# The sort of the edges moved into the first convolution of a graph network, with other changes to scatters and small products

## The chip, the cores and the metric

One core of one Trainium2 chip runs the kernel. The metric is device time in microseconds, the median of several executions. A core has five engines that run their own instruction streams in order: TensorE (PE: matrix products into PSUM), VectorE (DVE), ScalarE (ACT), GpSimd (POOL) and SyncE (SP, which here only issues transfers). They meet through semaphores. Transfers are issued from the queues of SP, ACT and POOL and are carried out by 16 DMA engines.

## The reference

There are 12500 nodes with 64 features and 200000 edges, sorted by `dst`. Two GraphSAGE convolutions are followed by one edge network with a mean over the edges of each source node:

```python
h = relu(layernorm(x))
# twice, a relu between the two:
#   mean of h[src] over the edges of each dst, then  mean @ Wl.T + b + h @ Wr.T
x = x + conv2(relu(conv1(h)))
h = relu(layernorm(x))
# edge network
inp = concatenate([h[src], h[dst], edge_attr], axis=-1)
msg = relu(inp @ W1 + b1) @ W2 + b2
x = x + segment_mean(msg, src)
```

The kernel splits the first product of the edge network: `h[src] @ W1[0:64]` and `h[dst] @ W1[64:128]` are formed per node, and `edge_attr @ W1[128:192]`, the *edge terms*, per edge.

## The kernel before

**Blocks and cells.** The nodes are cut into NB = 49 blocks of 256. A *cell* is a pair (block of dst, block of src); there are 49 x 49 = 2401 cells, and a cell has room for S = 128 edges. For each cell the kernel holds the source's and the target's number inside its block. Gathering rows of a block is then a product with a one-hot matrix (`turned`, lines 640 to 650, made by VectorE from rows of numbers that are broadcast to all partitions), and summing over targets is another such product (`hot`, lines 652 to 661, made from columns of numbers).

**Start.** `find_blocks` finds for each block the window of the sorted edges that holds its own, `begin_i`. `features` (433) makes the layer norm of all nodes and splits it into three bf16 parts, the table `ta`. Meanwhile SP's queue gets transfers that write zeros into four tables `terms[0..3]` in DRAM (`zeros`, 250), 832 KB each.

**The sort** (`cells`, 464, in a pool scope of its own). `edges_in` (501) loads source and target numbers for seven blocks of dst at a time (14 transfers on SP's queue). `sort(B)` (536) does one block in five stages: one-hot of the source block for the window's 128 x 34 places (540), counts per column by 34 products (546), a running sum (550), the rank of each edge inside its cell by products with a triangular matrix (558, 559) and a minimum over PSUM (563), a compare of ranks with 0..127 (569), 34 products that put the numbers in place (579), three transfers of the result to DRAM (584 to 586), and a transpose for the column form (589 to 591). It also writes `pos`, the place in `terms` for each edge's term. Blocks are staggered: the loop at 599 runs the stages of several blocks in each turn. After 18 blocks it has issued all zeros and begins to run the edge terms beside the sort.

**The edge terms** (`edge_terms`, 321) come in *units* of up to four items, an item being 128 x 2 edges of one block: transposes (368), a copy by ACT (373), products with the weights (380), a copy by ACT into one of four buffers `terms_o` (388), and then one indirect scatter per item and half, on POOL's queue (345), into table `B % 4`. Blocks are taken four at a time, one for each table, and block 48 alone. In all there are 49 x 34 = 1666 scatters. A unit is emitted in six steps; `Beside` (394) holds a pace, and whoever calls `passed(us)` advances the steps that have come due. So the order of work is that of the program, written out by hand: each engine's queue gets instructions in the order in which the Python code emits them.

**The convolutions** (loop at 846). For `layer` 0 and 1, cells in order, 16 to a part, four to a turn. A turn calls `some_cells` (792): it emits the gather products of four cells (801), their copies into a ring of seven row buffers (805; `RB`, 269) and the one-hot of the targets (806); three turns later the sums' products (681) into the block's PSUM bank `acc`. After the last cell of a block `conv` (718) goes on: it copies the sums (722), forms the mean (726 to 734), transposes it and multiplies it by the weights in the bank `pX` (738, 744), and `after_conv1` or `after_conv2` finishes. Every turn also advances the edge terms: `beside.passed((z - a) * 0.37)` in layer 0, 0.375 in layer 1, against a pace of 10.4/6 for a step. `wait_rows` (634) loads the rows of a part, two parts ahead, through SP.

**The last stage** (loop at 972) gathers from both tables, adds the edge terms that come back from `terms`, applies relu, sums and finishes each node.

Of the kernel before, what the change touches and what calls it, by code (L numbers as in the profile page):

```python
# [9 lines left out]
FT = mybir.dt.float32  # L10
BF = mybir.dt.bfloat16
# [103 lines left out]
def fast_path(  # L115
# [39 lines left out]
    BIG = 1024.0  # L155
# [35 lines left out]

    per = EROWS * D // P
    ZW = per // NB
    zero = consts.tile([P, ZW], FT, name="zero")
    nc.gpsimd.memset(zero, 0.0)
# [54 lines left out]
    def zeros():  # L250

        n = 2
        for k in range(0, NB, n):
            m = min(n, NB - k)
            for j in range(J):
                nc.sync.dma_start(terms[j].rearrange("(p n r) d -> p n (r d)", p=P, n=NB)[:, k:k + m],
                                  zero.unsqueeze(1).to_broadcast([P, m, ZW]))
                yield

    clearing = zeros()  # L260
# [8 lines left out]
    RB = 7  # L269
# [51 lines left out]
    def edge_terms(work, psum):  # L321

        loads = []
        for q in (*range(BJ - 3), BJ - 1, BJ - 3, BJ - 2):
            blocks = range(q * J, min(q * J + J, NB))
            step = 3 if len(blocks) == J else 4
            loads += [(blocks, t0, min(step, TG - t0)) for t0 in range(0, TG, step)]

        def load(blocks, t0, m):
            n = len(blocks)  # L330
            e = work.tile([P, J, 3, 2 * D], FT, name="edges")
            ev = e.rearrange("p j c d -> p (j c) d").rearrange("p (a c) d -> p a c d", a=n if n == J else 1)
            for i, B in enumerate(blocks):
                s = nc.sync.value_load(begin_i[0:1, B:B + 1], min_val=0, max_val=E - WIN)
                a = edge[bass.ds(s, WIN)].rearrange("(p t) d -> p t d", t=T)
                nc.sync.dma_start(ev[:, i, 0:m].rearrange("p c d -> p (c d)"),
                                  a[:, 2 * t0:2 * (t0 + m)].rearrange("p t d -> p (t d)"))
            return ev

        def scatter(o, blocks, unit):  # L340
            for h in range(2):
                for c, (i, tg, _) in enumerate(unit):
                    B = blocks[i]
# [12 lines left out]
        for at, (blocks, t0, m) in enumerate(loads):  # L356
            n = len(blocks)
            ev = ahead

            if n == J:  # L360
                units = [[(i, t0 + c, ev[:, i, c]) for i in range(n)] for c in range(m)]
            else:
                units = [[(0, t0 + c, ev[:, 0, c]) for c in range(m)]]
            for u, unit in enumerate(units):
# [22 lines left out]
                o = work.tile([P, 4, 2, D], FT, name="terms_o", bufs=4)  # L387
                nc.scalar.copy(o[:, :k], pm[:, :k])
                before = scatter(o, blocks, unit)
# [43 lines left out]
    def features():  # L433
# [6 lines left out]
        with tc.tile_pool(name="in", bufs=3) as work:  # L440
            line = Line()
            for s in range(NB // CH):
                line.tick(some(work, s))
                next(finding, None)
                next(clearing, None)
                line.tick()
                next(finding, None)
                next(clearing, None)
            while line.all:
                line.tick()  # L450
                next(finding, None)
                next(clearing, None)
            for _ in finding:
                pass

    features()
    first.close()
    psum_x = ctx.enter_context(tc.tile_pool(name="psum_x", bufs=1, space=bass.MemoryType.PSUM))
# [3 lines left out]
    beside = Beside(edge_terms(terms_work, psum_x), 10.4 / 6)  # L462

    def cells():
        work = stage.enter_context(tc.tile_pool(name="cells", bufs=2))
# [780 lines left out]
```

## Time and profile before

| | us |
|---|---|
| median of 3 runs (4303.64 to 4310.11) | 4305.94 |
| the profiled execution | 4318.44 |
| its span, first to last instruction | 4316.5 |

A page of the profile begins with busy time per engine:

```
PE 3760.4 (87%) x50387; PEld 3550.8 (82%) x50387; DVE 3400.7 (79%) x6079; ACT 2487.0 (58%) x5687; POOL 2704.7 (63%) x2300
```

PEld is the loading of weights, which overlaps the products. The first gather product of the first convolution starts at 806.8 us of the span, that of the second at 1765.4, the last stage's first product at 2848.9. A group line of the profile reads: line, engine, operation, out<-in, shapes, count | busy us, mean ns of one | idle us ahead of them, and what ended that idle time. Rows of the sort's operations, from the stretch 0 to 830 us:

```
L579 PE MATMUL pC<-hot_r,hot 128*98 128x128 bf16 x1666 | 162.0, 282 | 16.9 <-ACT dcol L591 16.8
L569 DVE TENSOR_TENSOR hot_r<-rank_b,rexp 128x4352 bf16<-128x4352 bf16 x49 | 118.8, 2425 | 1.7
L563 DVE TENSOR_REDUCE rank<-pR 128x10 f32<-128x490 f32 x147 | 93.1, 663 | 87.4 <-PE pR L559 87.1
L558 PE MATMUL pR<-hot,lead 128*128 128x490 bf16 x147 | 75.4, 513 | 0.0
L559 PE MATMUL pR<-wide,ones 49*128 49x490 bf16 x147 | 74.8, 509 | 0.0
L546 PE MATMUL pH<-ones,hot 128*49 128x1 bf16 x1666 | 62.1, 172 | 83.1 <-DVE before L550 47.0 <-issue 36.0
L540 DVE TENSOR_TENSOR hot<-kv,kexp 128x1666 bf16<-128x1666 bf16 x49 | 50.0, 1020 | 52.7 <-PE pC L579 52.7
L558 PE MATMUL pR<-hot,lead 128*128 128x196 bf16 x49 | 15.5, 316 | 0.0
L559 PE MATMUL pR<-wide,ones 49*128 49x196 bf16 x49 | 15.4, 315 | 0.0
L589 PE MATMUL pC<-ident_b,rows_o 98*128 98x98 bf16 x49 | 12.6, 258 | 0.0
```

and of the edge terms, from 810 to 1760 us:

```
L380 PE MATMUL pE<-we,edges_t 128*128 128x128 f32 x675 | 91.9, 279 | 0.0
L368 PE MATMUL pE<-ident,edges 128*128 128x128 f32 x340 | 52.6, 277 | 4.0 <-ACT terms_o L388 4.0
L388 ACT COPY terms_o<-pE 128x512 f32<-128x512 f32 x85 | 51.0, 600 | 6.8 <-DMA terms<-terms_o,pos 6.4
```

### The profile page before, as it was taken

To read this page: it belongs to the slowest core of one execution; us is meant where nothing else is said; L and a number is where in the kernel's file an instruction comes from. 1 tells how busy PE (TensorE), PEld (TensorE's weight loads), DVE (VectorE), ACT (ScalarE), POOL (GpSimd) and SP (SyncE) were. 2 spreads that over 40 slices of the span, in tenths; PEclk is the share of its full clock that TensorE was granted. 3 is DMA by queue.
4 is the path that set the end of the run, shared out by engine and by line. 5 is a ranking of instruction groups with operands and counts; after the bars stand their busy time and mean duration, and the time that the engine had idled before them with its cause. 6 is when DMAs were issued, how large, how long until landed. Compare 5 with 4: busy or idle time off the path is not lost.

```text
span 4316.5 us, 124949 instructions
## 1 busy us (share of the span) xinstructions
PE 3760.4 (87%) x50387; PEld 3550.8 (82%) x50387; DVE 3400.7 (79%) x6079; ACT 2487.0 (58%) x5687; POOL 2704.7 (63%) x2300
## 2 busy tenths in 40 slices
PE   0767767699999999999998899979999989999997
PEld 0445545699999999999998799978898989888987
DVE  6878666477777777777776677879999999999997
ACT  2001111366666666667665566656676767776775
POOL 3008888777777777777775677725555555554554
PEclk9957666799999999999999899989999999999999
DMA  5971111343444344444443344355554545454552
GB/s 208 358 280 46 45 47 43 104 133 122 135 130 132 127 132 130 125 141 132 133 125 111 107 131 130 121 185 163 168 178 160 179 168 178 164 173 160 176 177 98
DMA packets 309532, 620.93 MB, mean 144 GB/s; under 512 B 74402, under 2 KB 158630, under 8 KB 308864
## 3 DMA queue, kind: packets, MB, share of 16 engines
q1 hardware_dynamic: 247572, 557.98, 39.3%
q0 software_dynamic: 53312, 51.36, 4.1%
q8 instruction: 396, 6.49, 0.6%
q10 hardware_dynamic: 8060, 3.53, 0.3%
q14 instruction: 192, 1.57, 0.1%
HBM read 465.04 MB, written 150.96 MB: 143 GB/s over the span
## 4 chain that ended last, share of the span: by engine, by line
PE 54%; issue 12%; DVE 11%; POOL 10%; DMA 4%; ACT 2%; SPq 1%; POOLq 0%; ACTq 0%; DVEq 0%
PE acc L681 20%; PE got L801 13%; POOL terms L345 10%; PE got L919 10%; PE got L920 5%; DMA terms<-terms_o,pos 3%; PE pE L380 3%; DVE turned_d L647 3%; DVE turned L647 2%; DVE hot L656 1%; PE pE L368 1%; DVE y L925 1%; DVE mean L880 1%; PE pX L744 1%; ACT rows L805 1%
## 5 line engine op out<-in xcount | busy, mean ns | idle before, releaser
L345 POOL DMA_INDIRECT terms<-terms_o,pos x1666 | 1898.3, 1139 | 803.0 <-issue 462.9
L805 ACT CAST rows<-got 128x384 bf16<-128x384 f32 x2402 | 1035.5, 484 | 578.8 <-PE got L801 568.4
L932 POOL TENSOR_TENSOR hidden<-hidden 128x512 f32<-128x512 f32 (+1 forms) x602 | 771.5, 1281 | 723.6 <-ACT hidden L929 700.0
L681 PEld LDWEIGHTS <-hot 128*128 128x128 bf16 x12006 | 1045.9, 99 | 46.3 <-issue 30.5
L681 PE MATMUL acc<-rows,hot 128*128 128x193 bf16 x9604 | 1008.8, 247 | 2.2 <-DVE hot L656 2.2
L647 DVE TENSOR_SCALAR turned<-srow,nid 128x2048 bf16<-128x2048 bf16 (+1 forms) x906 | 756.7, 849 | 124.7 <-PE got L801 116.7
L919 PE MATMUL got<-tb,turned_d 128*128 128x128 bf16 x4802 | 755.1, 223 | 85.6 <-DVE turned_d L647 85.6
L801 PEld LDWEIGHTS <-turned 128*128 128x128 bf16 x9604 | 813.2, 98 | 7.5 <-issue 6.3
L656 DVE TENSOR_TENSOR hot<-dcol,local 128x1024 bf16<-128x1024 bf16 x1202 | 798.1, 684 | 22.7 <-PE acc L681 22.1
L919 PE MATMUL got<-ta,turned 128*128 128x128 bf16 x4802 | 744.9, 223 | 23.2 <-DVE y L926 16.1
L920 PE MATMUL got<-tb,turned_d 128*128 128x64 bf16 x4802 | 686.2, 195 | 0.0
L920 PE MATMUL got<-ta,turned 128*128 128x64 bf16 x4802 | 678.8, 195 | 0.0
L919 PEld LDWEIGHTS <-turned_d 128*128 128x128 bf16 x4802 | 449.5, 100 | 101.3 <-DVE turned_d L647 97.5
L940 ACT ACTIVATE hot_a<-every,less 128x256 bf16<-128x256 bf16 x1200 | 507.7, 495 | 0.0
L801 PE MATMUL got<-ta,turned 128*128 128x192 bf16 x4802 | 495.4, 246 | 6.1 <-issue 5.8
L801 PE MATMUL got<-tb,turned 128*128 128x192 bf16 x4802 | 496.8, 247 | 0.0
L919 PEld LDWEIGHTS <-turned 128*128 128x128 bf16 x4802 | 450.6, 99 | 35.3 <-DVE y L926 27.3
L920 PEld LDWEIGHTS <-turned_d 128*128 128x128 bf16 x4802 | 447.1, 99 | 0.0
L920 PEld LDWEIGHTS <-turned 128*128 128x128 bf16 x4802 | 445.7, 99 | 0.0
L941 ACT ACTIVATE hot_a<-hot_a 128x1024 bf16<-128x1024 bf16 x300 | 317.5, 1058 | 9.5
L647 DVE TENSOR_SCALAR turned_d<-drow,nid 128x2048 bf16<-128x2048 bf16 (+1 forms) x302 | 309.7, 1068 | 1.9 <-DMA drow<-drow_k 1.9
L929 ACT ACTIVATE hidden<-y 128x512 f32<-128x512 f32 (+1 forms) x301 | 190.0, 631 | 206.2 <-DVE y L926 190.8
(206 smaller groups left out, 4912.8 us busy)
## 6 DMA issues: line engine op xcount, KB each, us to landing
srow<-srow_b SPq DMA_DIRECT2D x300, 512.0 KB
terms<-zero SPq DMA_DIRECT2D x96, 832.0 KB
srow<-srow_k SPq DMA_DIRECT2D x150, 512.0 KB
drow<-drow_k SPq DMA_DIRECT2D x150, 512.0 KB
terms_in<-terms SPq DMA_DIRECT2D x147, 384.0 KB
edges<-in_edge_attr_dram SPq DMA_DIRECT2D x240, 192.0 KB
terms<-terms_o,pos POOLq DMA_INDIRECT x1666
terms_in<-terms SPq DMA_DIRECT2D x49, 416.0 KB
```

Source lines behind the costliest of these rows:

```text
L345: nc.gpsimd.indirect_dma_start(out=terms[B % J][:], out_offset=bass.IndirectOffsetOnAxis(ap=pos[:, B, t:t + 1], axis=0), in_=o[:, c, h], i ...
L647: nc.vector.tensor_scalar(o[:, h, :n * S], r[:, :n * S], nid[:, h:h + 1], None, op0=OP.is_equal)
L656: nc.vector.tensor_tensor(o[:, :n], cols.rearrange("p (g c) -> p g c", c=2).unsqueeze(2).to_broadcast([P, n, 2 * P, 2]), local.rearrange(" ...
L681: nc.tensor.matmul(self.acc[B][:, h, :W3], lt, r[:, c, 0:W3], start=k + h == 0, stop=k == NB - 1 and h == 1, skip_group_check=True)
L801: nc.tensor.matmul(p[:, (i - c) * D3:(i - c + 1) * D3], t[:, h, (a - c0 + i) * S:(a - c0 + i + 1) * S], table[:, (a + i) % NB, h], start=h ...
L805: nc.scalar.copy(g[:, c:c + m, :D3], p[:, :m * D3].rearrange("p (c d) -> p c d", c=m))
L919: nc.tensor.matmul(p[:, c], lt, rt[:, 0:2 * D], start=i == 0, stop=False, skip_group_check=True)
L920: nc.tensor.matmul(p[:, c, 0:D], lt, rt[:, 2 * D:], start=False, stop=i == 3, skip_group_check=True)
L929: nc.scalar.activation(w[:, :n, 0:D], y[:, :n], AF.Relu)
L932: nc.gpsimd.tensor_sub(w[:, :n, (i + 1) * D:(i + 2) * D], w[:, :n, j], upper(w)[:, :n, j])
L940: nc.scalar.activation(q[:, c - k], every, AF.Abs, bias=less[(a + c) // NB][:, (a + c) % NB:(a + c) % NB + 1])
L941: nc.scalar.activation(q[:, :n - k], q[:, :n - k], AF.Relu, bias=1.0, scale=-2.0)
```

## The change

The sort has no stage of its own any more. `made_cells` is a generator of 12 steps a block; block 0 is sorted ahead of the first convolution, and the other 48 in its turns, by `sort_to(z)`, about one block per row of 49 cells and one to two blocks ahead. Its tiles have one buffer each, its PSUM is the one bank `pX`. The minimum over PSUM becomes four copies by ACT, two halving minima and one reduction by VectorE; the compare of ranks is done in two halves. The overflow check uses the counts.

Zeros: two tables are cleared at the start, all 50 transfers ahead of `features` in SP's queue; the other two are cleared in the first convolution, one transfer every eight cells. The zeros are now read from the end of `tb`, the table of the second convolution, which has moved to the constants.

Edge terms: none beside the sort. Blocks 0 to 11 are taken in pairs of two tables (0 and 1 first, then 2 and 3), the rest in fours, the last five together. The buffers `terms_o` go from four to three, `RB` from seven to five. A turn passes 1.1 per cell in layer 0 and 0.9 in layer 1 against a pace of 3.64 for a step.

The small products of `conv` go into its own bank `acc`, behind the sums that have been copied out, and no longer into `pX`. Layer 1's temporary tiles come from a pool that is opened when the sort's is closed. Block 0's edge numbers are loaded through ACT's queue.

```diff
+    tb = consts.tile([P, NB, 2, D3], BF, name="tb")
-    zero = consts.tile([P, ZW], FT, name="zero")
-    nc.gpsimd.memset(zero, 0.0)
+    ZB = -(-ZW // D3)
+    nc.vector.memset(tb[:, NB - ZB:], 0.0)
+    zero = tb[:, NB - ZB:].rearrange("p b h d -> p (b h d)").bitcast(FT)[:, :ZW]
...
-    def zeros():
+    def zeros(tables):
...
-            for j in range(J):
+            for j in tables:
...
-    clearing = zeros()
+    EARLY = 2
+    clearing = zeros(range(EARLY))
...
-    RB = 7
+    RB = 5
...
     def edge_terms(work, psum):
+        groups = [[q, q + 1] for q in range(0, 3 * J, J)] + [[q + 2, q + 3] for q in range(0, 3 * J, J)]
+        groups += [[*range(q, q + J)] for q in range(3 * J, NB - 1 - J, J)]
+        q = NB - 1 - J
+        groups.append([q, q + 1, q + 4, q + 2, q + 3])
+        ITEMS = 12
         loads = []
-        for q in (*range(BJ - 3), BJ - 1, BJ - 3, BJ - 2):
-            blocks = range(q * J, min(q * J + J, NB))
-            step = 3 if len(blocks) == J else 4
+        for blocks in groups:
+            step = ITEMS // len(blocks)
             loads += [(blocks, t0, min(step, TG - t0)) for t0 in range(0, TG, step)]
...
+            items = [(B, t0 + c, e[:, i * m + c]) for c in range(m) for i, B in enumerate(blocks)]
+            units = [items[u:u + 4] for u in range(0, len(items), 4)]
...
-                o = work.tile([P, 4, 2, D], FT, name="terms_o", bufs=4)
+                o = work.tile([P, 4, 2, D], FT, name="terms_o", bufs=3)
...
+    for _ in clearing:
+        pass
     features()
     first.close()
+    clearing = zeros(range(EARLY, J))
...
         def sort(B):
...
+            nc.vector.tensor_tensor(v[:, :, 0], mid(pairs(kv), NB), lead_(kexp, TG), op=OP.is_equal)
+            yield
+            many = psum.tile([P, 512], FT, name="pX")
             for g in range(TG):
                 for c in range(2):
-                    nc.tensor.matmul(many[:, 2 * g + c:2 * g + c + 1], v[:, g, 0, :, c], ones[:, 0:1],
+                    nc.tensor.matmul(many[:NB, 2 * g + c:2 * g + c + 1], v[:, g, 0, :, c], ones[:, 0:1],
                                      start=True, stop=True)
+            nc.vector.tensor_tensor_scan(b[:, 1:T + 1], flat_ones, many[:NB, :T], 0.0, op0=OP.mult, op1=OP.add)
             yield
...
+            for n, g0 in enumerate(range(0, TG, 5)):
+                yield
...
+                nc.tensor.matmul(q, lead, flat(v[:, g0:g1, 0]), start=True, stop=False)
+                nc.tensor.matmul(q, ones[:NB], flat(w[:, g0:g1]), start=False, stop=True)
+                nc.scalar.copy(flat(r[:, g0:g1]), q)
+                if n < 2:
+                    nc.vector.tensor_mul(v[:, :, n + 1], v[:, :, 0], mid(pairs((slo, dlo)[n]), NB))
             yield
+            k = NB
+            for _ in range(2):
+                h = k - k // 2
+                nc.vector.tensor_tensor(r[:, :, 0:k - h], r[:, :, 0:k - h], r[:, :, h:k], op=OP.min)
+                k = h
+            nc.vector.tensor_reduce(pairs(rank), r[:, :, 0:k].rearrange("p g k c -> p g c k"), AX.X, OP.min)
...
+            for n, (g0, g1) in enumerate(((0, (TG + 1) // 2), ((TG + 1) // 2, TG))):
+                hot = work.tile([P, (TG + 1) // 2, S, 2], BF, name="hot_r", bufs=1)
+                nc.vector.tensor_tensor(hot[:, :g1 - g0], mid(pairs(rb)[:, g0:g1], S), lead_(rexp, g1 - g0),
+                                        op=OP.is_equal)
+                yield
...
+    STEPS = 12
+    sorted_to = [0]
...
+    sorter = made_cells(sorting.enter_context(tc.tile_pool(name="cells", bufs=2, side="right")), psum_x)
+    while sorted_blocks() < 1:
+        next(sorter)
+
+    def sort_to(a):
+        while sorter is not None and sorted_to[0] < STEPS * (1 + min((a + 4) / 14, 1 + (a + 12) / NB)):
+            if next(sorter, sorter) is sorter:
+                break
+
+    beside = Beside(edge_terms(terms_work, psum_x), 3.64)
...
     def conv(layer, table, w, b, finish, B, acc):
...
-        pt = psum_x.tile([P, 4, P], FT, name="pX")
         for h in range(2):
-            nc.tensor.transpose(pt[:, h], m[:, h].rearrange("p a d -> p (a d)"), ident)
+            nc.tensor.transpose(acc[:, h, :P], m[:, h].rearrange("p a d -> p (a d)"), ident)
...
-        po = psum_x.tile([P, 8, D], FT, name="pX")
         for h in range(2):
-            nc.tensor.matmul(po[:, h], ct[:, h], w, start=True, stop=True)
+            nc.tensor.matmul(acc[:, h, P:P + D], ct[:, h], w, start=True, stop=True)
...
+    sort_to(0)
+    filled = 0
...
             line.tick(some_cells(layer, t, c0, a, z))
+            if layer == 0:
+                sort_to(z)
+                while filled < z:
+                    filled += 8
+                    next(clearing, None)
             next(coming, None)
-            beside.passed((z - a) * (0.37, 0.375)[layer])
+            beside.passed((z - a) * (1.1, 0.9)[layer])
...
+        if layer == 0 and c1 == CELLS:
+            for _ in chain(sorter, clearing):
+                pass
+            sorting.close()
+            second[0] = layers.enter_context(tc.tile_pool(name="second", bufs=2))
```

## The prediction

> **What bounds the kernel now.** I began with the busy rows of the page, then the table of busy time by stretch, then the scatters (line 345) by stretch, then the waits, then the timeline. The busy rows, in 40 slices of 108 us:
>
> ```profile
> PE   0767767699999999999998899979999989999997
> POOL 3008888777777777777775677725555555554554
> GB/s 208 358 280 46 45 47 43 104 133 122 135 130 132 127 132 130 125 141 132 133 125 111 107 131 130 121 185 163 168 178 160 179 168 178 164 173 160 176 177 98
> ```
>
> There are three regimes: zeroing and sorting (to 324 us), sorting with scatters (to 807), the rest. The table by stretch (us; PE, PEld, DVE, ACT, POOL busy; clock; DMA share; GB/s):
>
> ```profile
> 324.00:807.00 483.00, 332.65 (x2916) 244.18 (x2915) 299.32 (x444) 68.12 (x182) 390.66 (x303) 0.67 0.19 48
> 807.00:1765.00 958.00, 953.38 (x10906) 945.22 (x10906) 700.73 (x1384) 658.78 (x1611) 742.15 (x684) 1.00 0.42 129
> 2306.00:2414.00 108.00, 72.96 (x717) 69.73 (x715) 51.08 (x118) 46.91 (x127) 37.36 (x35) 0.81 0.29 88
> 2849.00:4316.00 1467.00, 1324.82 (x24157) 1289.05 (x24155) 1366.05 (x2038) 1008.52 (x1899) 771.45 (x602) 0.97 0.50 167
> ```
>
> The stretch from 807 to 1765 is the first convolution; PE is full there. POOL looks 77% busy, but its group lines for 430 to 800, 807 to 1765 and 2306 to 2414 say otherwise:
>
> ```profile
> L345 POOL DMA_INDIRECT terms<-terms_o,pos x238 | 298.9, 1256 | 72.6 <-issue 70.4 <-DMA terms<-terms_o,pos 1.2 <-ACT rows_o L582 0.9
> L345 POOL DMA_INDIRECT terms<-terms_o,pos x684 | 742.8, 1086 | 216.0 <-issue 191.9 <-DMA terms<-terms_o,pos 10.4 <-ACT rows L805 8.2
> L345 POOL DMA_INDIRECT terms<-terms_o,pos x35 | 37.5, 1072 | 70.9 <-DMA terms<-terms_o,pos 58.1 <-ACT terms_o L388 5.8 <-issue 3.2
> ```
>
> In the second line 742.8 + 216.0 = 958.8 us: POOL has no free time, its idle time is 0.3 us of issue ahead of each scatter. In the first, 298.9 + 72.6 = 371 of 370. So from 324.1 us, where the first scatter starts, to about 2802, where the last ends, POOL runs one scatter after another: 1666 in 2478 us, 1.49 each (1.56 beside the sort, 958/684 = 1.40 in the first convolution, 541/375 = 1.44 in the second up to 2306). Whatever is done to the sort, the last stage (from 2849) can't begin before this queue is done. **So I count scatters, and check the other engines against that count.**
>
> Two things lengthen a scatter. Here one meets a long VectorE compare:
>
> ```profile
> 712.21 2.43 DVE L569 TENSOR_TENSOR hot_r<-rank_b,rexp 128x4352 bf16<-128x4352 bf16 x1
> 712.96 2.52 POOL L345 DMA_INDIRECT terms<-terms_o,pos  x1 [0.30 <-issue]
> 715.78 1.20 POOL L345 DMA_INDIRECT terms<-terms_o,pos  x1 [0.30 <-issue]
> ```
>
> The scatter, 0.97 us when free, ends 0.84 after the compare does (714.64): it stood still while the compare ran. The other is its table. From 2306 to 2414 block 48 is scattered alone, all into one table:
>
> ```profile
> 2311.69 0.97 POOL L345 DMA_INDIRECT terms<-terms_o,pos  x1 [1.46 <-DMA terms<-terms_o,pos]
> 2314.96 0.97 POOL L345 DMA_INDIRECT terms<-terms_o,pos  x1 [2.30 <-DMA terms<-terms_o,pos]
> 2319.54 1.09 POOL L345 DMA_INDIRECT terms<-terms_o,pos  x1 [3.61 <-DMA terms<-terms_o,pos]
> 2323.73 1.30 POOL L345 DMA_INDIRECT terms<-terms_o,pos  x1 [3.10 <-DMA terms<-terms_o,pos]
> ```
>
> Each waits until the one before it has landed. Start to start is 2.40 to 5.25 us, 3.16 on average over the 33 steps there. With four tables in turn this wait is 10.4 us in 684 scatters.
>
> **Head.** The 483 us with scatters and most of the 324 ahead go. Kept: features, zeros for two tables, block 0. Its first VectorE work is at 112 us today. Its steps now run in series: tests and counts 1.0 + 1.6 + 0.2 + 1.0, four rounds of rank products and copies at about 1.8, minima 1.4, two compares 1.3 each, 34 products 3.8, a copy 0.3: some 20 us, so 132. Then its row write, a row load (4.3 at 801.6) and the turning (1.4): about 142. Beside that, 50 zeroing transfers of 832 KB (41.6 MB) go ahead of the writes on SP; at the 358 GB/s of the second slice that is 116 us, at the 2.7 us an issue of the first 21 it is 137. I take 150 (140 to 165) for the first product of the convolution, and 163 for the first scatter, some 13 us of cells later: **161 us sooner than today**.
>
> **First convolution, POOL.** The pace gives 2401 x 1.1 / 3.64 = 725 steps, 121 units of six steps. The first six groups pair blocks of two tables: 12 blocks x 34 = 408 scatters, 54 units, the first 1074 cells; the other 67 units use four tables, 534 scatters.
> - Pairs: a scatter waits for the one two before it. Lower end: no wait, 1.46 (below). Upper end: one table, 3.16. In between, two slots of 1.41 give 2.82, so of each of block 48's 33 steps I take the larger of it and 2.82, and halve the mean: 1.66. For the first 400 cells, 152 of the 408, the other 50 zeroing transfers run as well; landings wait behind them, and I take 2.05 there, between 1.66 and 3.16, nearer the first since a transfer of 2.3 us (832 KB at 358 GB/s) comes once in about 6. Together 152 x 2.05 + 256 x 1.66 = 737, 1.80 each.
> - Four tables: 1.40, plus the sort's compares. Beside the sort the scatter took 1256 ns against 972 free, 0.28 more, with a block every 12 us or so; here a block takes 49 cells, about 31 us: 0.28 x 12/31 = 0.11, but the longest compare is cut in halves, so 0.06. 534 x 1.46 = 780. Ends: 1.40 and 1.56, 748 to 833.
>
> POOL: 1517 us. **The others in that stretch.** PE: 953 + 48 blocks at (62.1 + 75.4 + 74.8 + 15.5 + 15.4 + 162.0 + 12.6)/49 = 8.5 us in the sort's slow clock, 5.7 if scaled by its 0.67, so 274 to 409, + 36 more units at (52.6 + 91.9)/85 = 1.7, 61: 1288 to 1423. DVE: 701 + 48 x 9.2 (four passes at 1.02, the compare 2.43, minima of 816 and 408 elements at that rate 0.75 and a reduction 0.6 for the PSUM reductions' 2.35, small ones 1.0, the ids 0.38) = 1142. ACT: 659 + 48 x 3.1 + 36 x 1.2 = 851. All are under POOL, which hides them; if that cover were gone, PE alone would set 1290 to 1420.
>
> **Second convolution.** 1666 - 942 = 724 scatters x 1.46 (1.44 there, the last 170 in a five-block group of distance two to three at 1.5) = 1057. Block 48's stretch, 108 us for 35 that take 50 elsewhere, is gone; that is in the count. The pace ends 22 of 593 steps ahead of the end, 89 cells at 0.37 = 33, and 22 us lead over to the last stage, as from 2827 to 2849 now.
>
> **Sum.** 163 + 737 + 780 + 1057 + 33 + 22 = 2792 against 2849: -57. The last stage's 1467 us is untouched. Span 4316.5 - 57 = 4259; the profiled execution is 4318.4, 12.5 over the median of 4305.9, so the median becomes **about 4250**.
>
> **Edits at nothing.** Conv products in the bank of sums: they free the shared bank for the sort; a bank is needed again 49 cells later and is held some 24. Five row buffers for seven: read three turns after filling, two to spare. Three buffers of terms for four: POOL still has two units, 16 scatters, 23 us of work queued when ACT waits. On SP the sort's three writes a block, 14 id loads every seven blocks (11 us from 99.4 to 110.4) and the zeros go between the row loads, which are issued 16 to 32 cells ahead, 10 to 20 us; if that were used up, six bursts cost at most 66 us. Block 0's ids on ACT's queue have nothing behind them but its own copies; the zeros' memset on VectorE replaces 0.8 us on POOL.
>
> **The skill against the rows.** The Trainium skill's page "SBUF — State Buffer", section "Who interferes with whom", says that a VectorE instruction with two SBUF inputs blocks a GpSimd instruction that reads SBUF for its whole length, which the row at 712.96 agrees with and which speaks against moving the sort's compares beside more scatters. The same section infers that such an instruction does not hold up descriptor generation; by that the 0.06 would vanish and the first convolution be 32 us shorter. The measured row decides.
>
> **Rivals.**
> 1. *Pairs do not wait*: landings come faster since row loads are spread over longer cells. For: at 2.40 us two slots nearly cover a landing. Against: 17 of the 33 steps above exceed 2.82. 408 x 1.46 = 596, 141 less: 4110.
> 2. *Pairs wait more, slower*: in the first 1074 cells landings queue behind zeros and row loads until POOL's pairs cost more than the early start gave. It decides from 1.80 + 57/408 = 1.94 each; at 2.15, which is 3.0 during the zeros and 1.66 after, +143: 4390. For: in the first convolution the DMA share is 0.42 against 0.29 in block 48's stretch. Against: longer cells spread it.
> 3. *The sort's waits set PE*: twelve steps a block bounce among PE, ACT and VectorE. From 0.4 us a step (48 x 12 = 576 steps; 1517 - 1288 = 229) PE outlasts POOL; at 0.7, 1288 + 403 = 1691 us, 174 more: 4425. Against: steps are four cells, over 2 us, apart.
> 4. *It does not overlap*: the sort merely runs between cells, 958 + 48 x 13.2 = 1592, 75 more than POOL's: 4325.
>
> **Chances.** Forecast (pairs at 1.6 to 1.94, 4170 to 4297) 0.47; rival 1 0.13; rival 2 0.23; rivals 3 and 4 0.10; the rest, 0.07, is within 0.2% (8.6 us), about what a measurement of this kernel can tell from no change. So faster 0.60, slower 0.33. The range, 4110 to 4400, reaches to rivals 1 and 2; the forecast's own is 4170 to 4297.
>
> **What would show it.** First product of the convolution near 150 us; scatters from about 163; idle time of POOL put down to landings large in the first 1074 cells, about 100 to 250 us, and small after; the first convolution about 1500 us with PE near 85%; no dip for block 48; the last stage starting near 2790 and 1467 long. Wrong if POOL has free time in the first convolution (rival 3), or if a pair's scatter is at 1.46 or above 1.94.

## The result, and the profile after

| | us |
|---|---|
| before, median | 4305.53 |
| after, median of 4 runs (4492.04 to 4515.86) | 4507.68 |
| ratio, 95% interval | 1.0464 [1.0434, 1.0493] |
| the profiled execution's span | 4506.5 |

The changed kernel is 202 us slower, and 108 us above the end of the forecast range. One group of experiments below ran beside a run of the kernel before that took 5148 us in place of 4306, so their times stand for nothing outside that group.

Where the time went, from the first gather product of each stage (us from the start of the span):

| | before | forecast | after |
|---|---|---|---|
| first convolution's first product | 806.8 | 150 | 156.1 |
| first scatter | 324.1 | 163 | 186.7 |
| second convolution's first product | 1765.4 | | 1907.8 |
| last scatter ends | 2802.5 | | 3008.0 |
| last stage's first product | 2848.9 | 2792 | 3042.6 |
| last stage, to the end | 1467 | 1467 | 1464 |

The first convolution starts 651 us sooner and ends 142 us later: it takes 1752 us where it took 959. The second takes 1135 from first product to the last stage where it took 1083. The rows of busy tenths of the kernel after, 40 slices of 113 us:

```profile
PE   0576788778888888889999988989999999999997
POOL 3155677777888888777777776645555555555554
GB/s 282 261 211 194 104 85 87 74 72 97 78 96 80 96 89 85 101 126 122 129 128 120 131 125 117 122 124 200 157 178 175 171 170 168 176 165 169 168 176 102
```

The stretch that filled slices 2 to 8 before, at 6 or 7 tenths of PE, is gone, but the first convolution, slices 3 to 17 now, is at 6 to 8 tenths where it had 9. The table of busy time by stretch (us; PE, PEld, DVE, ACT, POOL; granted clock; DMA share; GB/s) for pairs of tables, four tables in the first convolution, and the second:

```profile
187.00:1041.00 854.00, 645.42 (x6874) 581.13 (x6875) 513.18 (x979) 372.02 (x924) 553.11 (x409) 0.87 0.37 122
1041.00:1908.00 867.00, 723.51 (x7921) 657.42 (x7920) 573.46 (x1099) 432.78 (x1069) 710.79 (x512) 0.92 0.29 89
1908.00:3018.00 1110.00, 1018.78 (x11109) 985.60 (x11108) 789.06 (x1812) 715.58 (x1914) 828.39 (x747) 0.98 0.40 126
```

From 1041 to 1908 no engine but POOL comes near to full: PE 83%, VectorE 66%, ACT 50%. The group lines of the scatters (line 352) in the same three stretches say why POOL is full (count | busy us, mean ns | idle us ahead, by what ended it):

```profile
L352 POOL DMA_INDIRECT terms<-terms_o,pos x409 | 554.0, 1355 | 387.8 <-DMA terms<-terms_o,pos 188.2 <-issue 97.9 <-ACT rows L825 93.3
L352 POOL DMA_INDIRECT terms<-terms_o,pos x512 | 711.3, 1389 | 156.5 <-issue 148.2 <-ACT rows L825 4.0 <-DMA terms<-terms_o,pos 1.9
L352 POOL DMA_INDIRECT terms<-terms_o,pos x747 | 829.3, 1110 | 271.9 <-issue 196.5 <-DMA terms<-terms_o,pos 58.7 <-ACT rows L825 9.8
```

In the first line 87.0 of the 387.8 us of idle time lie ahead of the first scatter, before the stretch; landings of earlier scatters ended 188.2 of the rest. In the second line 711.3 + 156.5 = 867.8 us of 867: the scatters still follow each other without free time, and the idle time is the 0.3 us of issue. So the count of scatters still sets the time; what changed is one scatter's mean, 1389 ns there against 1086 in the first convolution of before. It is no even lengthening. The timeline of VectorE, then of POOL, around one sorted block (start, duration, instruction; in brackets the idle time ahead and who ended it):

```profile
1513.06 0.22 DVE L556 TENSOR_TENSOR_SCAN before<-flat_ones,pX 49x34 bf16<-49x34 f32 x1 [2.73 <-PE pX L553]
1513.20 0.66 DVE L676 TENSOR_TENSOR hot<-dcol,local 128x1024 bf16<-128x1024 bf16 x1
1513.79 1.01 DVE L559 TENSOR_TENSOR wide<-before,own 49x1666 bf16<-49x1666 bf16 x1
1514.72 0.15 DVE L560 TENSOR_TENSOR most<-most,before 49x1 f32<-49x1 f32 x1
1514.79 0.74 DVE L667 TENSOR_SCALAR turned<-srow,nid 128x2048 bf16<-128x2048 bf16 x1
1515.45 0.68 DVE L676 TENSOR_TENSOR hot<-dcol,local 128x1024 bf16<-128x1024 bf16 x1
1516.06 1.01 DVE L573 TENSOR_TENSOR hot<-hot,slo 128x1666 bf16<-128x1666 bf16 x1
...
1521.06 0.68 DVE L676 TENSOR_TENSOR hot<-dcol,local 128x1024 bf16<-128x1024 bf16 x1
1523.97 0.99 DVE L578 TENSOR_TENSOR ranks<-ranks 128x816 bf16<-128x816 bf16 x2 [2.23 <-ACT ranks L571]
...
1513.17 1.54 POOL L352 DMA_INDIRECT terms<-terms_o,pos  x1 [0.30 <-issue]
1515.02 7.57 POOL L352 DMA_INDIRECT terms<-terms_o,pos  x1 [0.31 <-issue]
1522.89 0.97 POOL L352 DMA_INDIRECT terms<-terms_o,pos  x1 [0.30 <-issue]
```

VectorE waits 2.73 us for the count products of line 553, has a backlog when they are done, and works it off from 1513.06 to 1521.74 with each instruction starting about 0.07 us before the one ahead of it has ended. The scatter that starts at 1515.02 takes 7.57 us in place of 0.97. It ends at 1522.59, 0.85 us after VectorE's run of instructions does, which is where VectorE has to wait for ACT. Counted over all scatters of the first convolution: 51 take more than 2.5 us and together hold POOL 257 us longer than 51 free ones of 0.97 (one to each of the 48 blocks, nearly). Of them 46, with 244 of the 257 us, overlap a run like this one, which begins with a block's running sum (line 556). In the first convolution of before there is none; beside its sort the longest took 3.54.

My theory after this was that these standing scatters are the miss (A). The rivals: the sort costs by the amount of VectorE's work, in whatever order (B); or the sort's waits make PE the bound (C, rival 3 of the forecast).

### The profile page after: what moved, and what is told of

Same layout as the page of the kernel before. It is cut to its first block, busy times and chain, and to the rows that moved or that the text cites. A ratio compares the mean times of both kernels' runs of the same rounds, so it can differ in the third digit from the quotient of the medians.

```text
span 4506.5 us, 125498 instructions
## 1 busy us (share of the span) xinstructions
PE 3757.1 (83%) x50387; PEld 3542.0 (79%) x50387; DVE 3347.6 (74%) x6124; ACT 2577.0 (57%) x5897; POOL 2899.4 (64%) x2299
## 4 chain that ended last, share of the span: by engine, by line
## 5 line engine op out<-in xcount | busy, mean ns | idle before, releaser
L352 POOL DMA_INDIRECT terms<-terms_o,pos x1666 | 2092.6, 1256 | 815.7 <-issue 442.0
L701 PEld LDWEIGHTS <-hot 128*128 128x128 bf16 x12006 | 1075.6, 101 | 76.6 <-issue 49.3
L701 PE MATMUL acc<-rows,hot 128*128 128x193 bf16 x9604 | 1062.4, 255 | 0.3 <-DVE hot L676 0.2
L821 PEld LDWEIGHTS <-turned 128*128 128x128 bf16 x9604 | 847.9, 101 | 21.8 <-DVE turned L667 15.8
L821 PE MATMUL got<-ta,turned 128*128 128x192 bf16 x4802 | 530.9, 257 | 14.6 <-DVE turned L667 14.6
L951 PEld LDWEIGHTS <-turned 128*128 128x128 bf16 x4802 | 450.1, 99 | 35.2 <-DVE y L958 27.2
L371 PE MATMUL pE<-ident,edges 128*128 128x128 f32 x833 | 157.7, 318 | 373.6 <-ACT terms_o L391 370.7
L952 PEld LDWEIGHTS <-turned 128*128 128x128 bf16 x4802 | 445.3, 99 | 0.0
L371 PEld LDWEIGHTS pE<-ident,edges 128*128 128x128 f32 x833 | 102.4, 158 | 402.4 <-ACT terms_o L391 396.1
L391 ACT COPY terms_o<-pE 128x512 f32<-128x512 f32 (+1 forms) x216 | 125.1, 579 | 404.9 <-DMA terms<-terms_o,pos 393.4
```

Of the source, the lines that this page charges most:

```text
L352: nc.gpsimd.indirect_dma_start(out=terms[B % J][:], out_offset=bass.IndirectOffsetOnAxis(ap=pos[:, B, t:t + 1], axis=0), in_=o[:, c, h], i ...
L371: nc.tensor.transpose(pt[:, c], a, ident)
L701: nc.tensor.matmul(self.acc[B][:, h, :W3], lt, r[:, c, 0:W3], start=k + h == 0, stop=k == NB - 1 and h == 1, skip_group_check=True)
L821: nc.tensor.matmul(p[:, (i - c) * D3:(i - c + 1) * D3], t[:, h, (a - c0 + i) * S:(a - c0 + i + 1) * S], table[:, (a + i) % NB, h], start=h ...
L951: nc.tensor.matmul(p[:, c], lt, rt[:, 0:2 * D], start=i == 0, stop=False, skip_group_check=True)
L952: nc.tensor.matmul(p[:, c, 0:D], lt, rt[:, 2 * D:], start=False, stop=i == 3, skip_group_check=True)
```

## The experiments

For each, "long" counts the scatters above 2.5 us between 190 us and the second convolution's first product, and "hold" is the sum of their durations less 0.97 us each, both worked out from the trace.

**First group.** The first leaves the scatters out, so its last stage adds zeros for the edge terms:

```diff
-nc.gpsimd.indirect_dma_start(out=terms[B % J][:], ...)
```

> The changed kernel without its 1666 scatters; the edge terms are left out of the result. Theory A: POOL's queue sets both convolutions, and without it the first convolution falls from 1752 us to what PE needs, 1290 to 1420, and the second to about 1000. Theory C, that the sort's waits between the engines set the first convolution: it stays above 1650.

It took 4067.49 us. The table of busy time by stretch, of its first and second convolution:

```profile
157.00:1551.00 1394.00, 1291.88 (x14954) 1174.16 (x14955) 1093.52 (x2103) 806.15 (x2016) 0.00 (x0) 0.99 0.34 113
1551.00:2580.00 1029.00, 993.32 (x11119) 969.59 (x11118) 778.43 (x1813) 712.38 (x1916) 0.00 (x0) 1.00 0.36 113
```

With the whole sort in it and no scatters the first convolution takes 1394 us, 93% of it busy on PE: theory C falls. PE's own sum is 1292, VectorE's 1094, ACT's 806. The 1394 us come from the group that stands by itself, but PE's granted clock is 0.99 there and the last stage takes 1461 us, as in the changed kernel (1464), so I use them below.

The other three of this group:

> The changed kernel with the counts' 34 products issued one step sooner and the running sum two steps after them, so that VectorE no longer stands at the running sum waiting for PE (59 us in 24 waits from 1000 to 2200 us). Theory A: after each such wait VectorE works off its backlog without a pause and one scatter per block stands still for about 7.5 us; 51 scatters over 2.5 us hold 257 us between 190 and 1900. If the wait makes the burst, these scatters go and the kernel takes 4250 to 4330. Theory B: it is the sum of VectorE's work beside the scatters that costs, wherever it stands: within 30 us of 4507.

> The changed kernel with one tiny reduction behind each target one-hot of the first convolution, which reads two elements of it: 600 instructions more on VectorE, each of which has to wait for the one before it and so opens a pause. Theory A: the pauses let the held scatters in, the scatters of 2.5 us and more go from about 51 to under 15, and the kernel gets faster in spite of 50 to 100 us more work on VectorE: 4280 to 4380. Theory B: more work on VectorE, same time or up to 60 us slower: 4500 to 4570.

> The changed kernel with only blocks 0, 1, 4 and 5 in pairs, and after that two blocks of tables 0 and 1 with two of tables 2 and 3 in each group, so that a table comes up every fourth scatter (the zeros come every seven cells to be done in time). The pairs' 408 scatters took 2.09 us each, with 0.27 us of waiting for the one two before after the zeros, more during them. Theory A (POOL's count sets the time): 272 scatters lose the wait of 0.27, 73 us, so 4400 to 4450. If the pairs' waits are hidden by something else: 4507 within 20.

They took 4972.72, 4965.93 and 5108.70 us. The changed kernel itself was not run beside them, so only the durations of their scatters are read here: with the instruction of `break_burst` not one scatter was long in 1876 us of the first convolution, against 27 (hold 87 us) in `late_scan` and 31 (172 us) in `regroup`. All three edits were run again, outside that group, with the changed kernel as a control.

**Control.**

> The changed kernel again, with nothing edited, beside the next three on the same chip. Both theories: 4500 to 4520 us, some 50 scatters of the first convolution above 2.5 us that hold about 257 us over a free scatter's 0.97 us. On a chip where the kernel before takes over 5000 us again, everything is only compared within this group.

4511.65 us, ratio to before 1.0472 [1.0442, 1.0503]; 48 long scatters, hold 236 us.

**A pause in the run of instructions.** Behind each table of ones, a maximum of one element a row, in the first convolution alone:

```diff
         o = hot(work, dcol[:, even(a, z)], 5)
+        if layer == 0:
+            tiny = work.tile([P, 1], FT, name="tiny")
+            nc.vector.tensor_reduce(tiny, o[:, 0, 0], AX.X, OP.max)
```

> A one-element-a-row maximum behind each table of ones in the first convolution, which must wait for the table. Theory A (one scatter per sorted block stands still while VectorE's instructions follow each other without a pause): no scatter above 2.5 us, 200 to 260 us less than the changed kernel, so 4250 to 4310. Theory B (the sort costs by the amount of VectorE's work, whatever its order): 425 instructions more on VectorE, so the same or up to 60 us more, 4500 to 4570.

4367.65 us, 1.0138 [1.0109, 1.0168]: 144 us less than the control, with 601 instructions more on VectorE (one for each turn of four cells, not the 425 I wrote). One long scatter of 2.50 us is left of the 48. VectorE's and POOL's timeline around one block:

```profile
1379.81 0.22 DVE L556 TENSOR_TENSOR_SCAN before<-flat_ones,pX 49x34 bf16<-49x34 f32 x1 [2.31 <-PE pX L553]
1379.95 0.66 DVE L676 TENSOR_TENSOR hot<-dcol,local 128x1024 bf16<-128x1024 bf16 x1
1380.64 0.15 DVE L829 TENSOR_REDUCE tiny<-hot 128x1 f32<-128x2 bf16 x1
1380.71 1.01 DVE L559 TENSOR_TENSOR wide<-before,own 49x1666 bf16<-49x1666 bf16 x1
...
1382.38 0.68 DVE L676 TENSOR_TENSOR hot<-dcol,local 128x1024 bf16<-128x1024 bf16 x1
1383.09 0.15 DVE L829 TENSOR_REDUCE tiny<-hot 128x1 f32<-128x2 bf16 x1
1383.16 1.02 DVE L573 TENSOR_TENSOR hot<-hot,slo 128x1666 bf16<-128x1666 bf16 x1
...
1380.41 1.19 POOL L352 DMA_INDIRECT terms<-terms_o,pos  x1 [0.30 <-issue]
1381.90 1.41 POOL L352 DMA_INDIRECT terms<-terms_o,pos  x1 [0.30 <-issue]
1383.61 1.41 POOL L352 DMA_INDIRECT terms<-terms_o,pos  x1 [0.30 <-issue]
1385.33 0.97 POOL L352 DMA_INDIRECT terms<-terms_o,pos  x1 [0.30 <-issue]
```

The same wait, the same backlog, but the maximum has to wait for its table: it starts 0.03 us after that has ended (1379.95 + 0.66 = 1380.61, then 1380.64), where other instructions start 0.07 early. The scatters beside it take 1.2 to 1.4 us. So theory A holds and B falls; whether it is the pause comes below. The gain is 144 and not the expected 200 to 260. In the four tables' part the scatter still takes 1200 ns where before had 1086, as each is still held for an instruction or so, and in the pairs' part the scatter became 0.19 us shorter but only 0.12 came out, since the table's turn took up the rest.

**An instruction that need not wait,** in the same place:

```diff
+            nc.vector.memset(tiny, 0.0)
```

> The same place, but a one-element-a-row fill that reads nothing and so need not wait for the table. If what frees the scatter is VectorE's pause for a result of its own (A1): the long scatters stay, 4490 to 4540. If any short one-operand instruction in between frees it (A2): no scatter above 2.5 us, 4250 to 4310, as with the maximum.

4431.91 us, 1.0287 [1.0227, 1.0347]; 36 long scatters, hold 119 us, the longest 7.03. Neither expectation is met: it makes half the effect of the maximum. The fills start while the instruction ahead of them still runs (571 of 601 do), so they make no pause. So the maximum may help by its pause, or by being another kind of instruction, with one small operand. Two more kernels, run last, tell these apart. One has the pause with two operands, the other the one operand with nothing to wait for:

```diff
+            nc.vector.tensor_tensor(tiny, o[:, 0, 0, 0:1], o[:, 0, 0, 1:2], op=OP.max)   # dep_two
+            nc.vector.tensor_reduce(tiny, ident_b[:, 0:2], AX.X, OP.max)                 # free_max
```

> Behind each table of ones of the first convolution, a maximum of two single columns of that table (two operands in SBUF, must wait for the table) in place of the maximum along a row (one operand, must wait). If VectorE's pause lets the scatter go on (A1): no more than 3 scatters above 2.5 us, 4350 to 4390 us, as with the maximum along a row. If it is the instruction with one small operand (A2): the hold stays above 100 us and the time above 4410, as with the fill.

> The same place, a maximum along two elements of a constant table (one operand, nothing to wait for). A1, the pause: no pause, so the hold stays above 100 us and the time above 4410. A2, the instruction with one small operand: no more than 3 scatters above 2.5 us, 4350 to 4390.

`dep_two` took 4365.52 us, 1.0130 [1.0100, 1.0159], and no scatter of its first convolution is long. `free_max` took 4467.41, 1.0366 [1.0335, 1.0398], with 47 long scatters and a hold of 182 us. In `dep_two` the small instruction starts 0.035 us after its table has ended, in `free_max` 0.08 us before. It is the pause that lets the long scatters go: with the kind of instruction alone 47 of 48 stayed. Why the fill still took away half of the hold, and the maximum without a pause 54 us of it and 44 us of the time, is not settled.

**The counts' products sooner,** so that VectorE does not wait at the running sum:

```diff
             nc.vector.tensor_tensor(v[:, :, 0], mid(pairs(kv), NB), lead_(kexp, TG), op=OP.is_equal)
-            yield
             many = psum.tile([P, 512], FT, name="pX")
             ...
+            yield
+            yield
             b = before[B % 2]
             nc.vector.tensor_tensor_scan(b[:, 1:T + 1], ...)
-            yield
             ...
```

The running sum now stands in the same step as the table `wide` (line 559), which reads it.

> The 34 count products one step of the sort ahead of the running sum, on a chip that runs the kernel before at its usual 4306 us. If VectorE's backlog behind its wait for those products makes the long scatters: their number and hold fall by half or more from 48 and 236 us, so 4350 to 4410 us, and VectorE's wait in front of the running sum is gone from the waits. If they come from the wait for the copied ranks or from elsewhere: hold above 180 us, 4450 to 4520.

4414.79 us, 1.0238 [1.0205, 1.0272]: 97 us less than the control, 5 above the upper end of the first expectation. 32 long scatters, hold 100 us: the hold fell by 58%, the number by a third and not by half. The waits of the control's VectorE from 1000 to 1900 us (us, times, longest) begin so:

```profile
DVE ranks L578 <- ACT ranks L571: 72.4, 21, 10.1
DVE before L556 <- PE pX L553: 53.6, 24, 3.8
```

and those of this kernel so, from 1000 to 1860:

```profile
DVE ranks L578 <- ACT ranks L571: 62.9, 21, 8.2
DVE turned L667 <- PE got L821: 45.7, 26, 9.1
```

The wait at line 556 is gone, the one for the copied ranks is not. But the long scatters that are left do not come from that other wait. A timeline of this kernel, VectorE and then POOL:

```profile
1024.12 0.21 DVE L557 TENSOR_TENSOR_SCAN before<-flat_ones,pX 49x34 bf16<-49x34 f32 x1
1024.37 1.02 DVE L559 TENSOR_TENSOR wide<-before,own 49x1666 bf16<-49x1666 bf16 x1
...
1025.56 5.09 POOL L352 DMA_INDIRECT terms<-terms_o,pos  x1 [0.30 <-issue]
```

`wide` starts 0.04 us after the running sum has ended, and a run without a pause begins there. In the control 42 of the 48 long scatters (217 of the 236 us) overlap the run that begins with the running sum after its wait, 7.61 us long in the median; here 29 of the 32 (94 of the 100 us) overlap the run that begins with `wide`, 5.43 us in the median. Runs of over 6 us in the first convolution fell from 53 to 31. The runs that begin at line 578, behind the copied ranks, are at most 0.65 us long in both kernels. So the wait made the run longer, but the same work of the sort and the convolution makes a run without it.

**Fewer pairs.** Only the first four blocks are scattered with two tables:

```diff
-        groups = [[q, q + 1] for q in range(0, 3 * J, J)] + [[q + 2, q + 3] for q in range(0, 3 * J, J)]
-        groups += [[*range(q, q + J)] for q in range(3 * J, NB - 1 - J, J)]
-        groups.append([q, q + 1, q + 4, q + 2, q + 3])
+        groups = [[0, 1], [4, 5]]
+        groups += [[q, q + 1, q - 6, q - 5] for q in range(8, 48, J)]
+        groups.append([48, 42, 43, 46, 47])
...
-                    filled += 8
+                    filled += 7
```

> Only the first four blocks in pairs: 272 scatters get four tables. If a table's turn sets the pairs' period: these 272 go from 1.95 us to the four tables' 1.68, 70 us less, and the new last group of five (tables 2 and 3 twice) gives up to 20 back: 4435 to 4470. If the sort's instructions alone set the period there: 4490 to 4520.

4478.18 us, 1.0386 [1.0365, 1.0406], 33 us less, 8 above the upper end of the first expectation. The 272 scatters went from 1.96 to 1.74 us, 60 us, the last 169 from 1.69 to 1.76, 12 us back. The last scatter ended 46 us sooner (2956.1 for 3002.6), the last stage began 31 us sooner, since the gather products of 77 cells still followed the last scatter where 35 did. The long scatters stayed (50, hold 265 us). A table's turn cost, but far less than the standing scatters.

**All three.**

> Three edits at once: the maximum behind each table of ones; the counts' products one step of the sort sooner than the running sum that reads them; and only the first four blocks in pairs, so that 136 scatters instead of 408 have two tables. Theory A: 230 to 260 us from the scatters that stood still, and 272 scatters at about 1.45 in place of 1.95 us, about 110 us to 135 us more: 4120 to 4180. Theory B: the pairs' part alone, 4380 to 4450.

4300.37 us, 0.9986 [0.9966, 1.0006]: no different from the kernel before, and 120 us above the upper end of the expectation. The pairs gave 90 us of the 110 to 135 (the 272 scatters at 1.50 for 1.83), but the pause gave 144 where I had put 230 to 260, and the last scatter, 96 us sooner than with the pause alone, brought the last stage only 75 us sooner: the gather products of 77 cells, 29 us, came after the last scatter, where it was 21 cells.

**The last blocks,** in the kernel before and in the three edits. In before, block 48 goes with the last four:

```diff
-        for q in (*range(BJ - 3), BJ - 1, BJ - 3, BJ - 2):
-            blocks = range(q * J, min(q * J + J, NB))
-            step = 3 if len(blocks) == J else 4
+        last = NB - 1 - J
+        for blocks in [[*range(q, q + J)] for q in range(0, last, J)] + [[last, last + 1, last + 4, last + 2, last + 3]]:
+            step = 12 // len(blocks)
...
```

> The kernel before with one edit: its 49th block's 34 scatters, which it issues alone to one table, go together with the last four blocks. If one table's turns at 2.9 to 3.1 us each stop POOL's queue there: about 50 to 60 us less, 4245 to 4260. If the queue has slack there: 4300 to 4310.

4267.02 us, 0.9898 [0.9882, 0.9915]: 43 us less, of 50 to 60. The scatters' group line from 2306 to 2414, where before had 35 at 3.1 us each:

```profile
L345 POOL DMA_INDIRECT terms<-terms_o,pos x75 | 84.0, 1120 | 25.3 <-issue 21.0 <-ACT rows L803 2.4 <-DMA terms<-terms_o,pos 1.6
```

Part came back at the end: the last 169 scatters, now in a group of five with a table used twice, take 1.71 us where they took 1.41. The changed kernel has the same group, with 1.69. And the 43 us are not block 48's stretch alone. The last scatter ended 23 us sooner (2779.5 for 2802.5), the last stage began 49 us sooner (2800.1 for 2848.9). In both it begins 24 us after the second convolution's last gather product. In before the gather products of 53 cells, 22 us, followed the last scatter; here the terms make 213 units in place of 209, so the pace spreads them over more cells (24 steps of 1.73 at 0.375 a cell are 111), and none follows. In the three edits, the last thirteen blocks dealt so that no unit uses a table twice:

```diff
-        groups += [[q, q + 1, q - 6, q - 5] for q in range(8, 48, J)]
-        groups.append([48, 42, 43, 46, 47])
+        groups += [[q, q + 1, q - 6, q - 5] for q in range(8, 44, J)]
+        groups += [[44, 38, 39], [48, 42, 43], [45, 46, 47]]
...
-            units = [items[u:u + 4] for u in range(0, len(items), 4)]
+            w = 3 if len(blocks) == 3 else 4
+            units = [items[u:u + w] for u in range(0, len(items), w)]
...
-    beside = Beside(edge_terms(terms_work, psum_x), 3.64)
+    beside = Beside(edge_terms(terms_work, psum_x), 3.6)
```

> The three edits together once more, and the last thirteen blocks dealt as one group of four and three of three in which no two share a table, in place of two of four and one of five. If the last 169 scatters at 1.76 us wait for a table's last write: 1.42 to 1.48 here, 45 to 55 us less than the 4300 of the three edits, 4240 to 4265. If the queue's end is set by PE's share of the second convolution: 4290 to 4310.

4257.78 us, 0.988 [0.9863, 0.9898]: faster than both kernels, 43 us less than the three edits and 254 less than the control. The time is in the first expectation's range, its mechanism is not what made it. The last 169 scatters take 1.64 us, not 1.42 to 1.48: a turn of three tables still waits. And the last scatter ends where it did (2770.95 for 2771.18 us); the last stage begins 37 us sooner because no cell's gather products follow the last scatter, where 77 cells' did. Units of three items make 222 units of 214, and the pace is 3.6 for 3.64: both place the terms differently against the cells. Group lines of the scatters from 2490 to 2770, first of the three edits, then of this kernel:

```profile
L351 POOL DMA_INDIRECT terms<-terms_o,pos x158 | 177.4, 1123 | 100.8 <-DMA terms<-terms_o,pos 54.5 <-issue 33.3 <-ACT rows L824 6.3
```

```profile
L351 POOL DMA_INDIRECT terms<-terms_o,pos x173 | 190.4, 1101 | 91.4 <-issue 35.3 <-DMA terms<-terms_o,pos 27.6 <-ACT terms_o L391 14.5
```

The wait for landings is halved, and 14.5 us of waiting for terms of three items to a copy came in its place. How much of the 43 us the dealing gives without the other two is not known.

## Why the prediction was wrong

| term | forecast | after | with the pause (`break2`) |
|---|---|---|---|
| first scatter | 163 | 186.7 | 189.0 |
| 408 scatters in pairs | 737 | 854.0 | 803.8 |
| four tables, to the second convolution | 780 (534 of 1.46) | 867.7 (512 of 1.69) | 770.7 (512 of 1.51) |
| the rest | 1057 (724 of 1.46) | 1099.6 (746 of 1.47) | 1104.0 (746 of 1.48) |
| to the last stage | 55 | 34.6 | 31.7 |
| sum | 2792 | 3042.6 | 2899.2 |

The miss is 251 us: 24 at the first scatter, 117 in the pairs, 88 with four tables (and 22 scatters fewer there), 43 in the rest, 20 back at the end.

**Right: the bound.** POOL's queue of 1666 scatters sets the pace of both convolutions before and after; with four tables its idle time stayed at the 0.3 us of issue, and the last stage was untouched (1464 for 1467). Landings ended 188.2 us of POOL's idle time in the pairs, in the 100 to 250 that were forecast, then 1.9 with four tables in the first convolution and 58.7 in the second. The first product of the convolution (156.1 for 150) and PE's sum (1292 without scatters, for 1288 to 1423) were right too, VectorE's (1094 for 1142) and ACT's (806 for 851) near. The bound of before is also confirmed from its own side: without block 48's stretch alone in one table the last scatter came 23 us sooner (`before_five`).

**Wrong: the term "the sort's compares", 0.06 us a scatter.** I took one hold a block, as long as one compare, from the row at 712.96 of before, and scaled the 0.28 us of before's sort by the rate of blocks. (The 12 us a block in that sum are misread: the 23 compares from 431.0 to 750.5 us come every 14.5, so it should have been 0.13 and not 0.11 ahead of the halving.) After, a scatter with four tables took 1.69 us, 0.29 and not 0.06 over the 1.40; with the pause of `break2` it took 1.51. One scatter a block stood still through a whole run of instructions, 5 us longer than a free one on average (257 / 51), in the pairs as in the four tables. VectorE's share does not show it: 62% in before's sort (299.32 of 483), 60% and 66% in the two stretches after. Its runs do. Counting instructions that each start before the one ahead has ended, before's sort, from 324 to 807 us, has one run of over 4 us, of 4.01; after, from 187 to 1908 us, there are 78, the longest 9.60, and 56 of them over 6; in `break2`, from 993 to 1763, there is none, the longest 2.78. The forecast asked how long the longest instruction is and how often a block comes, and not whether VectorE would pause between its instructions, the sort's and the convolution's, once they come in turn; so halving the compare could not help (none of the 51 long scatters meets one, line 587, and 47 meet line 559 or 573), and the upper end, before's 1.56, was no bound. Of the 251 us between forecast and trace, the pause in `break2` removes 143 (144 of the median). The Trainium skill's page "SBUF — State Buffer", section "Who interferes with whom", says that a port pair is held for the whole of an instruction, and that a reduction on this chip never takes part; here a scatter stood through ten instructions, and a reduction put between them (`free_max`) left 47 long scatters where the control has 48.

**Also too small,** and left when the pause is in: the first scatter, 24 us late (the first product 6 us, the cells ahead of the scatter 31 us for 13); the pairs, 1.97 us each with the pause for 1.80, so 67 us more than forecast, and landings ended 227.0 us of the idle time there; and the last group of five, which I put at 1.5 and which took 1.66 in the changed kernel and 1.75 in `break2`, 27 and 42 us for its 169. The second convolution's other scatters were a little faster than forecast, 1.42 us for 1.44.

**The rivals.** Rival 2 (pairs wait more, deciding from 1.94 each) had the right sign: the pairs took 2.09. But its mechanism, landings that come late, is the smaller part of the miss: `few_pairs`, which does away with two thirds of the pairs, wins 33 us alone, while 88 us were lost where there are four tables and almost no wait for landings (1.9 us in the second group line). Inside the pairs it is the larger part: of their 117 us the pause removes 50 and 67 stay. Rival 3 fell with `no_scatter`: PE's 1394 us lie under POOL's count. Rival 4 fell with it, since 1394 is not 1592. Rival 1 was far off.

**Left open.** Why a scatter goes on at some of VectorE's overlapped changes of instruction and not at others. I count the changes of instruction inside scatters of over 1.1 us that leave more than 0.75 us of the scatter, and call a change passed when the scatter runs on for over 1.15 us. In the first convolution of the control 363 of 573 overlapped changes passed, and none of 40 with a pause. In before, from 190 us to the second convolution, only 33 of 219 overlapped ones passed, and its first convolution has 32 runs of over 4 us (none over 5.1) beside which no scatter took more than 2.17. The kinds do not explain it: from `hot` (line 676 after, 656 before) to the next instruction 144 of 234 passed in the control, 22 of 91 in before. In these kernels a long hold thus came only with a run without a pause, but not every such run made one, and no kernel was run that separates what else differs.

## What to carry to other kernels

Work that is moved beside a queue of indirect scatters is priced by the runs of VectorE instructions without a pause that it makes, not by its busy time or its longest instruction: look for the run, and put a short instruction that must wait for its predecessor into it (144 us here); to take away the wait ahead of it shortened the run and won 97. Where one engine's queue is full from end to end, count its instructions, ask of each neighbour what it does to one of them, and measure that where the neighbour's work comes as it will after the change. Deal successive scatters over four tables: with two, and still with three, some wait for a landing. Look also at what follows the queue's last instruction: of the last gains here, 26 of 49 us and all of 37 came from gather products that no longer followed it.

## What the runs showed of the hardware

- A scatter of 0.97 us when free stood still for 7.57 us through ten VectorE instructions, though all of them end in between; the longest in the changed kernel's first convolution took 9.34.
- A VectorE instruction that must wait for the one ahead started 0.035 us after its end (median of 601) and took about 0.16 us; with one operand or two, it took the long scatters from 48 to 1 and to none, and 144 and 146 us off the kernel.
- A one-element fill that reads nothing took 0.06 us, began while the instruction ahead of it still ran (571 of 601), and took the hold from 236 to 119 us; a maximum that had nothing to wait for took it only to 182.
